# Post-norm attention and ternary feed-forward in one kernel: transpositions over the full array, and the second batch's maxima split one, two, one

## The chip, the cores and the metric

The kernel runs on one core of a Trainium2 chip. The metric is device microseconds (us) of one execution of the program. Five engines work side by side, each through its own instructions in order: TensorE (PE in the profile; its weight loads are listed as PEld), VectorE (DVE), ScalarE (ACT), GpSimd (POOL), and SyncE (SP), which here only issues DMAs. They meet through semaphores.

## The reference

Four batches of 512 tokens, width 512. Attention has 16 heads of 32 dimensions and one key/value head that all of them share; the feed-forward layer has 1408 hidden units and ternary weights.

```python
q = rotary((x @ Wq + bq) per head); k = rotary(x @ Wk + bk); v = x @ Wv + bv
scores = q k^T / sqrt(32); attn = softmax(scores); ctx = attn @ v
x = layernorm(x + ctx @ Wo + bo)
quantize(w) = clip(round(w / (mean|w| + 1e-8)), -1, 1)
hidden = sigmoid(x @ quantize(w1).T) * (x @ quantize(w2).T)
x = layernorm(x + hidden @ quantize(w3).T)
```

The mean in `quantize` is one over a whole weight matrix, so each matrix is read once for its mean and once more to be made ternary, on the chip.

## The kernel before

**Steps.** `T = D = 512` is cut into four chunks of 128 (`NC`, `NT`). A chunk `c` of the query columns holds four heads. The main loop (line 855) goes through 64 steps `n` = (batch `b`, chunk `c`, key tile `t`), 16 to a batch. In step n TensorE makes the scores of 128 keys against 512 queries for four heads (`scores`, two double-bank PSUM tiles `ps` of tag `sc`, with the row maximum subtracted by a second small product), ScalarE takes the exponential (`es`), and TensorE weighs the value rows with the `es` of the step before (`weigh`, into `acc`). The softmax denominators are a further product for the first batch (`count`, into the PSUM bank of tag `den`) and a sum on GpSimd (`total`) for the others.

**Maxima.** The row maxima have to be known ahead. `find_maxima(n + LEAD, ...)` makes them seven steps ahead: for batch 0 with `row_maxima`, for the others with `maximum`, which multiplies the head's queries `qr` with the keys `kr`, one 128x512 product per query chunk, and has VectorE reduce the result (`pmax` to `mx`). `maximum` takes a tile of tag `sc` for two chunks at once, and the single bank of tag `den` for one chunk alone (line 378). After the last chunk of a head group `spread` transposes the 128x16 maxima on TensorE (`pm`), takes them into two float parts (`m`) and sends them round through DRAM to `negm`.

**PSUM.** Tag `sc` has two buffers of two banks, `mm` two of one bank (projections `pk`, `pq`, transposes `pv`, `pm`, `pt`, and the products `po`, `gu` of the later stages), `acc` and `den` one bank each. A buffer is handed on only when its last reader is done, wherever in the program that reader stands: `normalize` copies the denominators out of `den` on ScalarE (`sums<-den`, line 496) some slots after the last `count`.

**Fill.** The engines' order is that of the program text (`pin`). Between the pieces of a step `fill.draw(us)` puts in work of other stages: the input projections of later batches (`project_in`, with the rotation on VectorE: four or five instructions `a`, shuffle, `pq`, `q`), the output projection of the batch before (`project_out`), and its feed-forward layer. Lists of small pieces (`late`, `middle`) come in at `due()`.

**Weights.** `quantize(n)` advances the ternary weights by n tiles: ACT takes the sign of the raw tile (`sgn`), DVE makes the tile of it (`raw<-raw,hi,sgn`), POOL stores it to DRAM (`w<-raw`) and loads the next raw tile. `sgn` lies in SBUF for steps up to 16 and in the PSUM bank `den` after that (line 210). The last tiles are stored just ahead of the first feed-forward product, whose weights (`wg<-w`) take over the buffers of the raw tiles.

**Which steps the loop's two branches take.** While the last batch's input projections are not done (line 876), a step has two pairs of chunks, `find_maxima(.., 0, 1)` and `find_maxima(.., 2, 3)`, both in tag `sc`, with the fill after them. From step 26 on the other branch runs: chunk 0, fill, chunks 1 and 2, fill, chunk 3. Steps 16 to 25 are those of the second batch (b = 1) that fall into the first branch.

## Time and profile before

| what | value |
|---|---|
| median of the runs (lowest, highest) | 672.95 us (667.65, 673.8) |
| the profiled execution itself | 669.15 us, of which the profile spans 667.4 us |
| clock granted to TensorE in it | 0.997 |
| PE busy | 641.6 us, 96% |
| DVE, ACT, POOL busy | 430.4, 282.7, 323.8 us |
| PE, DVE, POOL busy from 160 to 230 us | 66.66, 56.63, 55.97 of 70 us |

Steps 16 to 25 lie between 151.7 and 227.7 us of the profiled execution; the first feed-forward product starts at 239.43 us. In a line of the timeline the columns are the start in us, the time in us, the engine, the line in the kernel, the operation, output<-inputs, their shapes, how many were merged into the line, and in brackets the engine's idle time before it with what ended that. A helper records every operation, so the lines named are those of the helpers (L75, L80, L83, L86) and one goes by the names of the tiles. The clock granted is that of the whole span; per stretch it is in the table of windows.

### The profile page before, as it was taken

What the parts mean: (1) busy time and instruction counts of PE and PEld (TensorE: products, weight loads), DVE (VectorE), ACT (ScalarE), POOL (GpSimd) and SP (SyncE); (2) the same over time, 40 slices, a digit from 0 to 9 for tenths busy, and PEclk for the clock granted to TensorE, in tenths of its full rate; (3) what the DMA queues carried; (4) which work ended last, traced back from release to release, by engine and by line L of the source; (5) the groups of instructions that cost most, each with busy time, mean ns of one, the idle gap of its engine ahead of it and who ended that gap; (6) DMA issues with size and microseconds to landing.
All of it is one profiled execution on the core that took longest, in us unless ns stands there. A gap on an engine that the chain in (4) does not pass through costs nothing.

```text
span 667.4 us, 9352 instructions
## 1 busy us (share of the span) xinstructions
PE 641.6 (96%) x3194; PEld 355.4 (53%) x3194; DVE 430.4 (64%) x619; ACT 282.7 (42%) x441; POOL 323.8 (49%) x414
## 2 busy tenths in 40 slices
PE   8999999999999989999999899999999999999995
PEld 5233333443333445665556465654555685778884
DVE  2987765787886967676666856576535553464345
ACT  2474656564443645333244354232435421234213
POOL 2533344545987766467666265586575702202000
PEclk9999999999999999999999999999999999999998
DMA  8855668777675285454132357451231464237531
GB/s 276 287 170 202 207 193 271 229 242 259 185 235 188 86 263 169 133 179 149 49 106 76 112 163 219 132 157 37 68 105 59 135 222 138 80 110 217 184 105 63
DMA packets 60671, 107.78 MB, mean 162 GB/s; under 512 B 14592, under 2 KB 15360, under 8 KB 60624
## 3 DMA queue, kind: packets, MB, share of 16 engines
q1 hardware_dynamic: 51984, 80.57, 38.9%
q0 software_dynamic: 7920, 25.96, 11.7%
q10 hardware_dynamic: 720, 0.66, 0.3%
q8 instruction: 25, 0.41, 0.3%
q14 instruction: 22, 0.18, 0.1%
HBM read 84.06 MB, written 23.10 MB: 161 GB/s over the span
## 4 chain that ended last, share of the span: by engine, by line
PE 78%; DVE 8%; DMA 5%; ACT 3%; POOL 2%; issue 2%; SPq 1%; ACTq 0%; DVEq 0%; POOLq 0%
PE gu L80 23%; PE po L80 19%; PE ps L80 12%; PE pmax L80 8%; PE acc L80 7%; PE pq L80 6%; DVE mx L75 2%; PE den L80 2%; ACT es L75 2%; DMA xT<-in_xT 2%; POOL total L75 1%; DVE xt L75 1%; DMA wg<-w 1%; DMA bq_sb<-in_bq 1%; DVE part L75 1%
## 5 line engine op out<-in xcount | busy, mean ns | idle before, releaser
L75 DVE TENSOR_REDUCE mx<-pmax 128x1 f32<-128x512 f32 (+1 forms) x159 | 158.2, 1006 | 80.7 <-PE pmax L80 80.4
L75 ACT ACTIVATE es<-ps 128x1024 f32<-128x1024 f32 x128 | 124.2, 1022 | 142.3 <-PE ps L80 134.2
L80 PE MATMUL gu<-y,wg 128*128 128x512 f32 x704 | 172.8, 395 | 1.9 <-DMA wg<-w 0.9
L80 PEld LDWEIGHTS gu<-y,wg 128*128 128x128 f32 x704 | 131.3, 188 | 37.9 <-issue 4.7
L75 POOL TENSOR_TENSOR total<-total,es 128x512 f32<-128x512 f32 x96 | 123.7, 1318 | 45.3 <-ACT es L75 45.2
L80 PE MATMUL po<-wd,h 128*128 128x512 f32 x352 | 87.1, 396 | 4.2 <-DVE y L75 2.9
L75 POOL TENSOR_TENSOR total<-es 128x512 f32<-128x512 f32 x48 | 60.5, 1290 | 56.8 <-ACT es L75 56.8
L80 PE MATMUL pmax<-kr,qr 128*128 128x512 f32 x192 | 75.5, 456 | 3.7 <-ACT es L75 2.2
L80 PEld LDWEIGHTS po<-wd,h 128*128 128x128 f32 x352 | 65.0, 188 | 22.5 <-DVE y L75 4.6
L75 ACT CAST h<-hw 128x512 fp32r<-128x512 f32 x44 | 27.3, 620 | 100.1 <-DVE hw L75 100.1
L80 PE MATMUL acc<-es,v 128*32 128x512 f32 x512 | 68.2, 605 | 0.0
L80 PEld LDWEIGHTS pmax<-kr,qr 128*128 128x128 f32 x192 | 33.7, 188 | 57.3 <-ACT es L75 21.2
L75 DVE SCALAR_TENSOR_TENSOR hw<-th,gu 128x512 f32<-128x512 f32 x44 | 30.2, 686 | 46.8 <-PE gu L80 46.6
L80 PE MATMUL po<-wo_sb,ctxT 128*128 128x512 f32 x128 | 58.9, 593 | 0.3 <-DVE hw L75 0.3
L80 PE MATMUL ps<-negm,ones_r 2*128 2x512 f32 x256 | 58.2, 788 | 0.0
L75 DVE SCALAR_TENSOR_TENSOR xt<-po,xt 128x512 f32<-128x512 f32 x48 | 32.8, 684 | 38.7 <-PE po L80 38.7
L75 DVE TENSOR_TENSOR h<-hw,h 128x512 fp32r<-128x512 f32 x44 | 42.2, 960 | 21.7 <-ACT h L75 21.4
L80 PE MATMUL ps<-qT,kT 32*128 32x512 f32 x384 | 55.7, 640 | 0.0
L75 POOL DMA_DIRECT2D raw<-in_wf x66 | 36.0, 548 | 37.7 <-DMA w<-raw 26.9
L80 PE MATMUL pq<-xT,wq_sb 128*128 128x512 f32 x112 | 53.0, 602 | 1.0 <-ACT v L75 1.0
L75 ACT ACTIVATE th<-gu 128x512 f32<-128x512 f32 x44 | 26.3, 597 | 49.3 <-PE gu L80 49.3
L80 PEld LDWEIGHTS po<-wo_sb,ctxT 128*128 128x128 f32 x128 | 24.1, 190 | 21.9 <-issue 19.6
(98 smaller groups left out, 632.5 us busy)
## 6 DMA issues: line engine op xcount, KB each, us to landing
wg<-w SPq DMA_DIRECT2D x88, 256.0 KB
raw<-in_wf POOLq DMA_DIRECT2D x66, 256.0 KB, 4.4
qr<-qp SPq DMA_DIRECT2D x96, 128.0 KB
wd<-w SPq DMA_DIRECT2D x44, 256.0 KB
w<-raw POOLq DMA_DIRECT2D x33, 256.0 KB, 4.9
qp<-q SPq DMA_DIRECT2D x48, 128.0 KB
rden<-flat SPq DMA_DIRECT2D x64, 64.0 KB
xt<-in_x SPq DMA_DIRECT2D x16, 256.0 KB
```

The lines of the kernel that those rows point to most:

```text
L75: return lambda *args, **kw: pin(getattr(self.engine, name)(*args, **kw))
L80: pin(nc.tensor.matmul(out, lhsT=lhsT, rhs=rhs, start=start, stop=stop))
```

## The change

Three edits:

1. `pv` and `pm` become transpositions over the full array. The value rows were transposed from partitions 96 to 127 alone (32 rows in, 128x32 out); now all 128 rows of `kv` are, 128x128 out, and the copy takes its 32 columns of each. For that `kv` is written on 128 partitions instead of 32. The maxima go to two constant 128x128 tiles, cleared once at the start, and `pm` transposes a whole one instead of its 16 columns.
2. `sgn` of the steps after 16 lies in SBUF, in bfloat16, in the one buffer of tag `rot_a`, instead of the PSUM bank `den`.
3. In steps 16 to 25 the maxima come as chunk 0 (bank `den`), then chunks 1 and 2 together (tag `sc`), and, after 0.3 of the step's fill, chunk 3 (bank `den`).

```diff
                 if now > PER:
-                    sgn = ps_acc.tile([P, W], F32, tag="den", name="sgn")
+                    sgn = work.tile([P, W], BF16, tag="rot_a", name="sgn", bufs=1)
...
         kv = work.tile([P, T], F32, tag="kv", name="kv", bufs=1)
-        act.activation(kv[n:P], pk[n:P], AF.Identity, bias=bkv_sb[n:P, 0:1])
+        act.activation(kv, pk, AF.Identity, bias=bkv_sb[:, 0:1])
...
-                pv = ps_mm.tile([P, NT, HD], F32, tag="mm", name="pv")
+                pv = ps_mm.tile([P, NT, P], F32, tag="mm", name="pv")
                 for t in range(NT):
-                    transpose(pv[:, t, :], kv[n:P, ts(t, P)], ident[n:P, n:P])
+                    transpose(pv[:, t, :], kv[:, ts(t, P)], ident)
                 s.v = work.tile([P, NT, HD], F32, tag="v", name="v", bufs=3)
-                act.copy(s.v, pv)
+                act.copy(s.v, pv[:, :, n:P])
...
+    maxima = [const.tile([P, P], F32, name=f"maxima{k}") for k in range(2)]
+    for tile_ in maxima:
+        pool.memset(tile_, 0.0)
+
+    def room_for_maxima(b, c):
+
+        return maxima[c % 2][:, 0 : NG * NT].rearrange("p (i t) -> p i t", t=NT)
...
-            s.mx[c] = small.tile([P, NG, NT], F32, tag="mx", name="mx")
+            s.mx[c] = room_for_maxima(b, c)
...
-        pm = ps_mm.tile([NG * NT, P], F32, tag="mm", name="pm")
-        transpose(pm, s.mx[c].rearrange("p i t -> p (i t)"), ident)
+        pm = ps_mm.tile([P, P], F32, tag="mm", name="pm")
+        transpose(pm, maxima[c % 2], ident)
+        pm = pm[0 : NG * NT]
...
-        if batches[-1].done < NC:
+        if b == 0:
             find_maxima(n + LEAD, 0, 1)
             begin_middle()
...
             fill.draw(pace)
-            quantize(1 if b == 0 or n % 3 == 0 else 0)
+            quantize(1)
+        elif batches[-1].done < NC:
+
+            find_maxima(n + LEAD, 0)
+            find_maxima(n + LEAD, 1, 2)
+            begin_middle()
+            due()
+            quantize(1)
+            fill.draw(0.3 * pace)
+            find_maxima(n + LEAD, 3)
+            fill.draw(0.7 * pace)
+            quantize(1 if n % 3 == 0 else 0)
```

More of the change, by code (lines that the diff above doesn't have):

```diff
@@ L375, in maximum @@
         if i == 0 and chunks[0] == 0:
-            s.mx[c] = small.tile([P, NG, NT], F32, tag="mx", name="mx")
+            s.mx[c] = room_for_maxima(b, c)
         if len(chunks) == 1:
```

## The prediction

> **What bounds the kernel.** I read the page's first part, then the waits, then the timeline of steps 16 to 27. TensorE is busy for 96% of the span, so a gain must come out of its idle time or its own work.

> ```profile
> PE 641.6 (96%) x3194; PEld 355.4 (53%) x3194; DVE 430.4 (64%) x619; ACT 282.7 (42%) x441; POOL 323.8 (49%) x414
> ```

> ```profile
> 160.00:230.00 70.00, 66.66 (x311) 25.32 (x311) 56.63 (x80) 33.84 (x48) 55.97 (x70) 1.00 0.56 181
> 230.00:240.00 10.00, 7.68 (x50) 4.02 (x47) 9.53 (x15) 5.97 (x9) 9.98 (x11) 1.00 0.79 249
> ```

> ```profile
> PEld pmax L80 <- ACT es L75: 15.6, 19, 1.1
> ```

> The second fence holds the windows of the steps that change and of the stretch behind them; after the length come PE, PEld, DVE, ACT and POOL busy, then the granted clock (1.00, so no term below is a matter of the clock). The last, from the waits of 150 to 240 us, names what the change goes at: the maxima's weight loads wait for the exponentials. Step 19 shows how:

> ```profile
> 177.90 1.06 PE L80 MATMUL acc<-es,v 128*32 128x512 f32 x8
> 179.13 0.73 PE L80 MATMUL pmax<-kr,qr 128*128 128x512 f32 x2 [0.17 <-ACT es L75]
> 180.05 0.74 PE L80 MATMUL pmax<-kr,qr 128*128 128x512 f32 x2 [0.18 <-ACT es L75]
> 180.63 1.88 PE L80 MATMUL pq<-xT,wq_sb 128*128 128x512 f32 x4
> ```

> Undisturbed, `acc` hands over after 0.88 us (127.54 to 128.42), and four `pmax` take 1.03 us (129.40 to 130.43), 0.26 each. Here 178.78 to 180.63 is 1.85: an excess of 0.82. Each pair waits for a `sc` bank, the first 1.08 us after the exponentials start, the second 2.00. The excess in steps 18 to 25 is 0.76, 0.82, 0.73, 0.72, 0.84, 0.83, 0.82 and 0.70, in sum 6.2. Step 16 has none, and in step 17 `pk` waits for an `xT` load that ends at 165.29 anyway.

> **Part 3, the split maxima.** Chunk 0 would start when `acc` is through, and the pair follows as soon as the first exponential frees its bank (about 0.1 later than chunk 0 ends). If nothing else held, eight steps would give 6.2 - 8 x 0.1 = 5.4 us. But both single chunks use the one bank `den`, so each needs the reduction of the one before, and VectorE takes those in program order. I laid each step's instructions on each engine in the changed order, with the durations of this trace, and found four places where the bank is late.

> Step 16: the last `count` stands directly ahead of chunk 0, and its copy `sums<-den` on ACT, behind two `es` and `ctxT`, ends at 156.23. Chunk 0 starts at 156.31 instead of 155.27: 1.04 lost, nearly all absorbed in step 17 by the `xT` wait. Step 18 starts 0.16 late.

> Steps 17, 18 and 19: chunk 3's reduction stands on VectorE behind a whole rotation.

> ```profile
> 167.21 0.75 DVE L75 SCALAR_TENSOR_TENSOR a<-pk,bkv_sb,cos_sb 96x512 f32<-96x512 f32 x1 [0.93 <-ACT kv L75]
> ...
> 169.40 1.38 DVE L75 TENSOR_TENSOR kT<-a,pk 96x512 f32<-96x512 f32 x2
> ```

> In step 17 the rotation ends at 170.78, the reduction (0.68) at 171.46, and step 18's chunk 0, wanted at 170.45, starts at 171.52: the whole gain of step 18 gone. In step 18 it ends about when step 19 wants it. In step 19 the reduction ends near 185.6, or 186.5 with the next part's cost, and step 20 wants the bank at 184.1: 1.4 to 2.4 lost. From step 20 on chunk 3's reduction stands ahead of the slow work, and steps 21 to 24 gain 0.6 to 0.8 each. In step 25 chunk 3 follows `pm` with no fill between, and waits 0.7 for chunk 0's reduction.

> VectorE also gets more to do: two reductions of 0.68 and one of 1.215 for two of 1.215, +0.145 a step, 1.45 in ten. The orders of ACT, POOL and SP stay as they are, so no DMA is moved past another; the later release of a `qr` buffer by chunk 3 (about 2 us) is hidden, since five buffers leave its next load two steps.

> **Part 2, signs in SBUF.** ACT's write costs 0.72 instead of 0.69. The reader is the matter: `raw` then has two tensor inputs in SBUF, as `h` has, and `h` shows what that does beside GpSimd.

> ```profile
> 259.13 5.03 POOL L75 TENSOR_TENSOR total<-total,es 128x512 f32<-128x512 f32 x4 [2.79 <-ACT es L75]
> ```

> ```profile
> 126.12 0.92 DVE L75 SCALAR_TENSOR_TENSOR raw<-raw,hi,sgn 128x512 f32<-128x512 f32 x1
> ...
> 203.09 0.74 DVE L75 SCALAR_TENSOR_TENSOR raw<-raw,hi,sgn 128x512 f32<-128x512 f32 x1
> ...
> 263.01 1.70 DVE L75 TENSOR_TENSOR h<-hw,h 128x512 fp32r<-128x512 f32 x1
> ...
> 536.32 0.69 DVE L75 TENSOR_TENSOR h<-hw,h 128x512 fp32r<-128x512 f32 x1 [0.69 <-ACT h L75]
> ```

> Alone `h` takes 0.69; under a running `total` it takes 1.70, one GpSimd instruction (1.24) longer. `raw` with `sgn` in SBUF took 0.92 next to a GpSimd product at 126.12; with `sgn` in PSUM it took 0.72 to 0.75 all through 160 to 229, though GpSimd was busy. Of the 12 `raw` after step 16, eight fall under `total`: between nothing and 8 x 1.1 = 8.8; I take 8 x 0.85 = 6.8, most `h` under `total` being near 1.7. VectorE's load from 160 to 230 then goes from 56.6 to 56.6 + 1.45 + 6.8 = 64.9 of 70 us. Most of that fills VectorE's waits for `pmax`; it shows on the path where a reduction or rotation queues behind it, in steps 19 to 20 (0.9) and 25 to 27 (1.4).

> **The sum of parts 2 and 3.** Starts of the score products against before, by step: 18 +0.2, 19 +0.2, 20 -0.5, 21 +1.2, 22 +0.8, 23 +0.1, 24 -0.7, 25 -1.4, 26 -1.0. Then VectorE, 9.53 of 10 us busy from 230 to 240, decides: its rotation starts 0.4 later than before, and TensorE's `pt` and scores go with it (+0.45). TensorE then waits 0.91 less for the first weights, since their chain (POOL `q` at 229.40, store at 230.62, load at 235.50) starts about 1.4 earlier. First `gu`: 239.0 instead of 239.43, -0.4. From there all is the same order as before, and TensorE-bound; the shift stays.

> **Part 1, full-width transpositions.** `pm` and `pv` become what `pt` is: weight load 140 ns for 88 and 136, matmul 273 for 272 and 222.

> ```profile
> 135.72 0.73 PE L80 MATMUL pmax<-kr,qr 128*128 128x512 f32 x2
> 136.29 0.27 PE L86 MATMUL pm<-ident,mx 128*16 128x128 f32 x1
> 136.31 0.71 PE L80 MATMUL pmax<-kr,qr 128*128 128x512 f32 x2
> ...
> 173.89 0.43 PE L86 MATMUL pv<-ident,kv 32*128 32x32 f32 x4
> ```

> The two `pmax` pairs with `pm` between take 1.14 up to `pq` (136.86), without it 1.03: 0.11 for a narrow `pm`. Four `pt` take 0.60 to 0.66, so about 0.11 apiece in a stream. `pm` is between nothing and 16 x 0.052 = 0.83 dearer; I take 0. Four `pv` take 0.43 and would take 0.60: at most 4 x 0.17 = 0.7, and I take 0.2, since in step 18 chunk 3 lies behind them and fills the wait for ACT's copy. A gain of the size of that copy's wait (0.35, twice) is the other end. `kv` on 128 partitions is 0.68 before and 0.69 by the row `r`; the two clearings (0.2 each) lie on POOL at the start, ahead of loads that the critical chain does not hold.

> [...]

> **Together** -0.4 + 0.2 = -0.2 us on the profiled 669.15, 668.95. The runs of before lie at 667.65, 669.15 (profiled), 672.95 and 673.8; their mean is 670.9, and I set the forecast on it: about 671, 2 below the median. The three runs scatter by 0.9%, so a change under 1% (6.7 us) can't be told from none.

> **Rivals.** (a) VectorE keeps up and the bank is free: the 5.4 come whole, with the last wait for weights shortened too, 669.15 - 5.4 - 0.9 = 662.9, up to 1% faster. For it: PE's wait is plain, and VectorE waited 6.9 us for `pmax` in 160 to 230. Against it: the rotation ahead of chunk 3's reduction in steps 17 to 19. Chance 0.17.
> (b) Slower, through VectorE as the bound of steps 17 to 27: at 8.8 instead of 6.8 for the signs its work is 66.9 of 70 us, and once the 3 us left are less than its own waits for `pmax`, 6.9 before, of which half stay, it sets the step: +0.4 to +4, or 669.5 to 673. It decides from about 1.0 us extra per `raw`, with two more on the path. Chance 0.25.
> (c) Chunk 3 waits at each step, because the fill draws less than VectorE needs for chunk 0's reduction: 0.7 as in step 25 in each of ten, +7, 676. Against it: two `pq` or `po` rows give 1.7. Chance 0.05.
> (d) The forecast, within about 2 of no change: 0.53.

> **Range and chances.** On the mean 670.9, (a) reaches to 665, (b) to 675; the runs' own scatter adds 2 above: 665 to 676, and the forecast's own range 668 to 674. Faster by over 1% is the far part of (a), 0.05; slower by over 1% is (c) and the end of (b), 0.08; within 1%, 0.87.

> **What would show it.** After: a wait of the first `pmax` of steps 18 and 20 that ends with VectorE's reduction, not with `es`; chunk 0 of step 16 behind `sums<-den`; `raw` at 1.4 to 1.8 where `total` runs; `po` of steps 21 to 23 half a microsecond behind the pair instead of 1.5 us behind `acc`; first `gu` near 239. I am wrong if VectorE's order lets the reductions pass earlier, if `raw` stays at 0.74, or if the narrow transpositions cost more than 0.11 by a wait that this trace puts down to other rows.

## The result, and the profile after

| | before | after |
|---|---|---|
| median of the runs (lowest, highest) | 668.99 us (667.42, 673.8), 22 runs | 672.19 us (668.89, 675.94), 22 runs |
| ratio, 95% interval | | 1.0040 [1.0025, 1.0055] |
| profiled execution, its span, its granted clock | 669.15, 667.4 us, 0.997 | 673.71, 671.9 us, 0.993 |

The change makes the kernel slower, by 2.7 us of 669 (1.7 to 3.7). The ratio is not that of the two medians; the means, 672.24 and 669.54 us, give it. The forecast was -0.2 us. The time measured lies between the 665 and 676 us that were given, but the change goes the other way.

The engines and the granted clock by slices, from the page of after:

```profile
PE 641.5 (95%) x3194; PEld 358.3 (53%) x3194; DVE 440.1 (65%) x629; ACT 283.1 (42%) x441; POOL 327.5 (49%) x416
...
PEclk9999999999979999999999999999999999999999
```

VectorE has 9.7 us more to do, TensorE as much as before, but one slice of the clock row shows a 7. The windows of after place it (length, then PE, PEld, DVE, ACT and POOL busy, then the granted clock, DMA share, GB/s):

```profile
160.00:230.00 70.00, 64.31 (x290) 26.71 (x289) 62.50 (x84) 31.48 (x44) 54.51 (x67) 0.95 0.55 174
230.00:240.00 10.00, 7.48 (x41) 3.26 (x40) 8.67 (x13) 6.58 (x10) 9.98 (x10) 1.00 0.51 148
...
184.10:187.50 3.40, 1.78 (x16) 0.32 (x10) 3.27 (x7) 2.42 (x3) 3.40 (x3) 1.00 0.27 103
187.50:194.30 6.80, 6.15 (x10) 3.20 (x11) 4.92 (x6) 1.24 (x2) 4.11 (x6) 0.50 0.71 198
194.30:197.70 3.40, 3.40 (x24) 1.06 (x22) 1.91 (x5) 0.56 (x1) 0.00 (x0) 1.00 1.01 374
```

From 187.5 to 194.3 us TensorE has half its clock, with 1.00 on both sides. TensorE's timeline of after, steps 16 to 21, shows what stands ahead of that:

```profile
156.27 0.96 PE L80 MATMUL pmax<-kr,qr 128*128 128x512 f32 x3 [0.93 <-ACT sums L75]
...
171.89 0.97 PE L80 MATMUL pmax<-kr,qr 128*128 128x512 f32 x3 [1.71 <-DVE maxima L75]
...
184.82 1.06 PE L80 MATMUL acc<-es,v 128*32 128x512 f32 x8
188.15 1.65 PE L80 MATMUL pmax<-kr,qr 128*128 128x512 f32 x3 [2.27 <-DVE maxima L75]
189.60 3.62 PE L80 MATMUL po<-wo_sb,ctxT 128*128 128x512 f32 x4
```

The waits of 150 to 240 us no longer have a row of `pmax` behind `es`. They have this one:

```profile
PEld pmax L80 <- DVE maxima L75: 13.2, 10, 3.2
```

So the waits for exponentials are gone, and waits for VectorE's reduction of the one bank stand in their place. In the timeline above, the third line from below is the last product before the wait of step 20; the `po` behind it takes 3.62 us, where four such products of `pq` at 172.69, at a clock of 1.00, took 1.88. VectorE's timeline of after shows what the reduction stood behind:

```profile
174.17 2.40 DVE L75 SCALAR_TENSOR_TENSOR raw<-raw,hi,sgn 128x512 f32<-128x512 f32 x1
...
183.40 1.25 DVE L75 SCALAR_TENSOR_TENSOR raw<-raw,hi,sgn 128x512 f32<-128x512 f32 x1
184.57 0.74 DVE L75 SCALAR_TENSOR_TENSOR a<-pq,bq_sb,cos_sb 128x512 f32<-128x512 f32 x1
...
186.81 0.69 DVE L75 TENSOR_TENSOR q<-a,pq 128x512 f32<-128x512 f32 x1
187.41 0.68 DVE L75 TENSOR_REDUCE maxima<-pmax 128x1 f32<-128x512 f32 x1
...
207.22 4.06 DVE L75 SCALAR_TENSOR_TENSOR raw<-raw,hi,sgn 128x512 f32<-128x512 f32 x1
```

The rotation, from `a` at 184.57 to `q`, stands right ahead of the reduction (`maxima`), with a `raw` ahead of both.

Starts of the score products against before, in us. The runs start up to 1.5 us apart for reasons of their own, so each row is taken from its own step 16:

| step | before, start | after | ten products in step 20's wait | signs made on ScalarE | the same, reduction first |
|---|---|---|---|---|---|
| 17 | 159.83 | +1.00 | +0.99 | +1.02 | +1.03 |
| 18 | 168.11 | -0.31 | +0.43 | +0.49 | +1.63 |
| 20 | 182.44 | +0.47 | -0.03 | -0.07 | +0.35 |
| 21 | 189.92 | +5.75 | +1.58 | +0.48 | -0.28 |
| 26 | 227.73 | +4.21 | +0.02 | -2.35 | -2.05 |
| first `gu` | 239.43 | +4.74 | +0.61 | -2.52 | -1.94 |

In the column of after little is lost up to step 20, 5.3 us between the starts of steps 20 and 21, and 1.5 is won by step 26.

### The profile page after: what moved, and what is told of

Read it like the earlier page. It is cut to its first block, busy times and chain, and to the rows that moved or that the text cites. A ratio compares the mean times of both kernels' runs of the same rounds, so it can differ in the third digit from the quotient of the medians.

```text
span 671.9 us, 9356 instructions
## 1 busy us (share of the span) xinstructions
PE 641.5 (95%) x3194; PEld 358.3 (53%) x3194; DVE 440.1 (65%) x629; ACT 283.1 (42%) x441; POOL 327.5 (49%) x416
## 4 chain that ended last, share of the span: by engine, by line
PE 80%; DVE 14%; DMA 2%; ACT 2%; issue 1%; ACTq 0%; DVEq 0%
PE gu L80 23%; PE po L80 19%; PE ps L80 12%; PE pmax L80 9%; PE acc L80 8%; PE pq L80 6%; DVE maxima L75 4%; PE den L80 2%; DVE raw L75 2%; DVE xt L75 1%; DVE part L75 1%; DMA bq_sb<-in_bq 1%; PE pk L80 1%; DVE y L75 1%; DMA xT<-in_xT 1%
## 5 line engine op out<-in xcount | busy, mean ns | idle before, releaser
L75 DVE TENSOR_REDUCE maxima<-pmax 128x1 f32<-128x512 f32 (+1 forms) x169 | 159.2, 955 | 79.2 <-PE pmax L80 78.9
L75 ACT ACTIVATE es<-ps 128x1024 f32<-128x1024 f32 x128 | 124.2, 1022 | 145.9 <-PE ps L80 138.6
L80 PE MATMUL gu<-y,wg 128*128 128x512 f32 x704 | 172.5, 395 | 1.9 <-DMA wg<-w 0.9
L80 PEld LDWEIGHTS gu<-y,wg 128*128 128x128 f32 x704 | 131.2, 188 | 37.3 <-issue 4.4
L75 POOL TENSOR_TENSOR total<-total,es 128x512 f32<-128x512 f32 x96 | 124.5, 1330 | 42.9 <-ACT es L75 42.8
L75 POOL TENSOR_TENSOR total<-es 128x512 f32<-128x512 f32 x48 | 61.4, 1309 | 60.7 <-ACT es L75 60.7
L80 PE MATMUL po<-wd,h 128*128 128x512 f32 x352 | 86.9, 395 | 4.2 <-DVE y L75 3.0
L80 PE MATMUL pmax<-kr,qr 128*128 128x512 f32 x192 | 78.3, 471 | 7.9 <-DVE maxima L75 6.9
L80 PEld LDWEIGHTS po<-wd,h 128*128 128x128 f32 x352 | 64.9, 188 | 22.3 <-DVE y L75 4.6
L75 ACT CAST h<-hw 128x512 fp32r<-128x512 f32 x44 | 27.3, 620 | 99.8 <-DVE hw L75 99.8
L80 PE MATMUL acc<-es,v 128*32 128x512 f32 x512 | 68.2, 605 | 0.0
L80 PEld LDWEIGHTS pmax<-kr,qr 128*128 128x128 f32 x192 | 35.0, 191 | 60.6 <-DVE maxima L75 19.4
L80 PE MATMUL po<-wo_sb,ctxT 128*128 128x512 f32 x128 | 61.8, 611 | 0.3 <-DVE hw L75 0.3
L75 DVE SCALAR_TENSOR_TENSOR hw<-th,gu 128x512 f32<-128x512 f32 x44 | 30.2, 686 | 46.7 <-PE gu L80 46.6
L75 DVE SCALAR_TENSOR_TENSOR xt<-po,xt 128x512 f32<-128x512 f32 x48 | 32.8, 684 | 38.6 <-PE po L80 38.6
L80 PE MATMUL ps<-negm,ones_r 2*128 2x512 f32 x256 | 57.8, 788 | 0.0
L75 DVE TENSOR_TENSOR h<-hw,h 128x512 fp32r<-128x512 f32 x44 | 42.0, 956 | 21.7 <-ACT h L75 21.4
L80 PE MATMUL ps<-qT,kT 32*128 32x512 f32 x384 | 56.2, 640 | 0.0
L75 POOL DMA_DIRECT2D raw<-in_wf x66 | 36.0, 548 | 36.8 <-DMA w<-raw 25.9
L80 PE MATMUL pq<-xT,wq_sb 128*128 128x512 f32 x112 | 53.2, 601 | 0.7 <-ACT v L75 0.5
L75 ACT ACTIVATE th<-gu 128x512 f32<-128x512 f32 x44 | 26.3, 597 | 49.2 <-PE gu L80 49.1
L80 PEld LDWEIGHTS po<-wo_sb,ctxT 128*128 128x128 f32 x128 | 24.9, 196 | 22.1 <-issue 19.1
```

What stands on the lines that cost most here:

```text
L75: return lambda *args, **kw: pin(getattr(self.engine, name)(*args, **kw))
L80: pin(nc.tensor.matmul(out, lhsT=lhsT, rhs=rhs, start=start, stop=stop))
```

## Experiments

The theory after the result: step 20's wait makes the granted clock fall, and both together take what the split maxima win. Rivals: the wider transpositions cost more than shown; the signs in SBUF alone do it; the split order in itself is worth nothing. Every ratio is to runs of before on the same chip, with its 95% interval.

### Each part alone

Before with edit 1 alone, with edit 2 alone, and with edit 3 alone (the signs then stay in `den`):

```diff
+        pm = ps_mm.tile([P, P], F32, tag="mm", name="pm")
+        transpose(pm, maxima[c % 2], ident)
...
+                    sgn = work.tile([P, W], BF16, tag="rot_a", name="sgn", bufs=1)
...
+            find_maxima(n + LEAD, 0)
+            find_maxima(n + LEAD, 1, 2)
```

> The kernel before with the full-width transpositions alone. Both theories (the granted clock falls after step 20's wait; or the waits alone make the loss) put nothing on this part: the scores of step 16 start at 151.69 us in the changed kernel and at 151.68 before, behind three of the four pv and six of the sixteen pm. Expected: ratio 0.999 to 1.001, pm at 0.27 us each, and the clock at 1.00 throughout. The rival that the transpositions cost what their weight loads and matmuls add would give +0.8 to +1.5 us, 1.001 to 1.002.

> The kernel before with the signs of steps after 16 in SBUF alone, maxima in two pairs as before. Raw tiles should take 1.2 to 2.4 us under total, in sum about 9 us more of VectorE's time between 160 and 230 us. Theory of the clock: the pairs' buffers are freed by the exponentials and the reductions of the step before, no wait of TensorE passes 2 us, the clock stays at 1.00, and the first gu is 0 to 1.5 us later: ratio 1.000 to 1.002. [...]

> Before, with only the split order of the maxima in steps 16 to 25; the signs stay in the den bank, the transpositions stay narrow. Of each step the single chunks now share den with the signs: ACT's sign pass waits for a reduction, and the next single chunk waits for raw. If signs in SBUF were a cost and no more, this order alone keeps the gain that the changed kernel with signs made on ScalarE showed: ratio 0.996 to 0.999, clock 1.00 in 185 to 196. If they are needed so that the split can work, chunk 0 of step 16 to 20 waits 1 us or more for den behind sign and raw, the clock falls at one of these waits, and the ratio is 1.002 to 1.010.

| kernel | median | ratio |
|---|---|---|
| transpositions alone | 670.05 us | 0.9999 [0.9979, 1.0020] |
| signs in SBUF alone | 671.0 us | 1.0021 [1.0002, 1.0039] |
| split maxima alone | 678.16 us | 1.0128 [1.0107, 1.0148] |
| all three | 672.19 us | 1.0040 [1.0025, 1.0055] |

The transpositions cost nothing that can be measured. In the profiled execution of the signs alone the twelve `raw` take some 5 us more, not the 9 expected, and the clock falls for 3.4 us at 236.1 us, where TensorE waits 1.22 and 1.07 us ahead of transpositions (against the expectation, which had it hold while no wait passes 2 us); the mean clock of its runs is 0.9935, that of before beside it 0.996. The parts don't add up: 0.0 + 0.2 + 1.3 is far above 0.4. The split order alone is the dearest, above both of its expected ranges, since signs and single chunks then share `den`. TensorE's timeline of the split maxima alone:

```profile
190.49 0.47 PE L80 MATMUL pmax<-kr,qr 128*128 128x512 f32 x1 [1.60 <-DVE raw L75]
...
233.36 0.77 PE L80 MATMUL pmax<-kr,qr 128*128 128x512 f32 x1 [3.73 <-DVE raw L75]
```

Chunk 3 waits for `raw` to have read the signs, seven times, by 0.48 to 3.73 us, and in the last of these waits, at 232.2 us, the clock falls for 6.8 us. So the signs in SBUF are dear by themselves (0.2%) and worth 0.9% beside the split maxima, which need `den` for themselves. I had priced that edit as a cost only.

### TensorE kept busy in step 20's wait

The changed kernel with ten 128x128 products that nobody reads, ahead of step 20's chunk 0:

```diff
+            if n == 20:
+                busy = ps_mm.tile([P, P], F32, tag="mm", name="busy")
+                for _ in range(10):
+                    mm(busy, ones, ones, True, True)
```

> The changed kernel with ten products of 128x128 into an unread tile ahead of step 20's first chunk: they keep TensorE at work for some 2.3 us of the time in which it waits for the bank. They leave the wait itself as it is: chunk 0 still starts at about 188.2 us. Theory of the clock: it stays at 1.00 in 185 to 196 us (0.69 in the changed kernel), step 21 starts at about 192.7 instead of 195.7, and the ratio falls from 1.004 to 0.999 to 1.001. Theory of the waits alone: nothing changes, 1.004, or worse by what the products delay.

Measured: 670.92 us, ratio 1.0016 [0.9997, 1.0035]. Its window over the same stretch of steps:

```profile
185.00:196.00 11.00, 11.00 (x56) 5.82 (x55) 9.99 (x15) 4.50 (x8) 8.26 (x10) 1.00 0.71 220
```

The clock stays at 1.00, and step 21 starts 1.58 us late where it was 5.75. The bank is still late, as TensorE's and VectorE's timelines of this kernel show:

```profile
183.03 1.07 PE L80 MATMUL acc<-es,v 128*32 128x512 f32 x8
184.03 2.50 PE L80 MATMUL busy<-ones 128*128 128x128 f32 x20
186.28 0.95 PE L80 MATMUL pmax<-kr,qr 128*128 128x512 f32 x3
```

```profile
185.18 0.68 DVE L75 TENSOR_REDUCE maxima<-pmax 128x1 f32<-128x512 f32 x1
```

The reduction ends at 185.86, 1.8 us behind `acc` where it was 2.2 in after, and the products end 0.4 later still. So what fell away is for the most part what the halved clock cost. The ratio is higher than expected: the mean clock over this kernel's runs is 0.994, so it falls in other runs too; where, no trace shows.

### Step 19's chunk 3 right behind its pair

```diff
+            if n == 19:
+                find_maxima(n + LEAD, 3)
             quantize(1)
             fill.draw(0.3 * pace)
-            find_maxima(n + LEAD, 3)
+            if n != 19:
+                find_maxima(n + LEAD, 3)
```

> The changed kernel with chunk 3 of step 19 alone put directly behind the pair, ahead of the fill, so that its reduction stands ahead of the rotation. Theory of the clock: step 20's wait for the bank (2.3 us) goes to under 0.4, the clock stays at 1.00, and step 21 starts 5 us earlier, near 190.5; ratio 0.996 to 0.999. Theory of the waits alone: 2.3 us are gained, less 0.3 for chunk 3's own wait, 1.001. If the clock falls at the next long wait instead (step 18's is 1.7 us), the ratio stays above 1.001 too, and the window shows where.

Measured: 670.47 us, ratio 1.0018 [0.9997, 1.0038]. Two of its windows:

```profile
185.00:196.00 11.00, 11.00 (x45) 5.01 (x45) 10.93 (x14) 5.41 (x9) 10.00 (x12) 1.00 0.67 216
230.00:240.00 10.00, 7.45 (x39) 3.73 (x39) 8.06 (x14) 4.55 (x7) 7.74 (x8) 0.83 0.84 259
```

Chunk 3 itself waits 0.32 us, step 20's wait is gone, and step 26 starts 1.5 us early by its own step 16. Then TensorE waits 1.38 and 1.07 us for the rotation and for `y` ahead of step 26's transpositions, and at 234.5 us the clock halves for 3.4 us. The gain was made, and given back a few steps on. Waits of 1.39 and 1.07 us stand at the same place in the executions of after and of the ten products, where the clock held. Over the twelve runs of this kernel the clock is no higher than in after (0.992 against 0.993), though step 20's wait is gone. So step 20 is not the only place where VectorE's lateness lowers the clock, and only one execution of each kernel shows where it fell.

### VectorE relieved, and VectorE put in another order

Four kernels run together. The first two make the ternary tile by two ScalarE passes (rounding by adding a large constant, then the sign), so that VectorE has no `raw` after step 16: on before, and on the changed kernel. The third issues chunk 3's product and reduction from within the fill, ahead of the rotation. The fourth is the second and third together.

```diff
-                    sgn = work.tile([P, W], BF16, tag="rot_a", name="sgn", bufs=1)
+                    act.activation(raw, raw, AF.Identity, bias=magic, scale=inv[m])
+                    act.activation(raw, raw, AF.Sign, bias=minus)
...
-                act.activation(sgn, raw, AF.Sign, bias=hi[m])
-                dve.scalar_tensor_tensor(raw, raw, hi[m], sgn, ALU.is_gt, ALU.min)
+                    act.activation(sgn, raw, AF.Sign, bias=hi[m])
+                    dve.scalar_tensor_tensor(raw, raw, hi[m], sgn, ALU.is_gt, ALU.min)
...
+            while pending:
+                pending.pop()()
             rotation = turn(
...
+            pending.append(lambda k=n + LEAD: find_maxima(k, 3))
             fill.draw(0.3 * pace)
-            find_maxima(n + LEAD, 3)
+            while pending:
+                pending.pop()()
```

> Before, with the ternary tiles behind step 16 made by two ACT passes in place, so that VectorE has no raw operation there and no tile of signs is needed: 12 VectorE instructions of 0.74 us less, ACT's pass for the sign is kept (0.69) and one more pass of about 0.7 us comes for each. It is the base for the next run: it shows what the ternary step costs in itself. Both theories (VectorE blocked by GpSimd; TensorE's wait that lowers the clock) expect nothing on the path: clock 1.00 in 160 to 240, steps 18 to 26 within 0.5 us of before, ratio 0.998 to 1.002. If ACT is the cover that is missing (56.6 less, 33.8 of 70 us busy before, so it should not be), steps come later by up to 0.7 each where an exponential queues behind the extra pass, 1.003 or more.

> The changed kernel, with the same two ACT passes in the place of raw: transpositions and split maxima as they are, but nothing on VectorE that reads two SBUF tiles for the ternary step (18.2 us of raw go from VectorE). If the signs' extra 9.3 us on VectorE are what made step 20's bank so late: TensorE's wait there falls from 2.4 to 1.4 us or less (the rotation of step 19 remains ahead of the reduction), the clock stays at 1.00 in 185 to 196, step 21 starts within 1 us of before instead of 5.8 late, steps 25 and 26 are 1 to 2 us early, ratio 0.995 to 1.000. If the order of the split maxima alone does it: the wait stays at 2 us or more, the clock falls, step 21 is 4 us or more late, ratio 1.002 to 1.006.

> The changed kernel, with chunk 3's product issued where TensorE has the fill's products behind it, but with its reduction on VectorE ahead of the rotation of that fill in steps 17 to 19 and later ones, signs in SBUF as they are. If the rotation ahead of the reduction is what makes the bank late: the waits of chunk 0 in steps 18 and 20 (1.71 and 2.27 us) go to 0.5 or less, the clock stays at 1.00 in 185 to 196, steps 21 to 26 come 0 to 2 us earlier than before, ratio 0.996 to 1.001. The rotation then ends 0.7 us later for each step, and may make the weights of steps 26 and 27 late: if a wait of 1 us or more stands there, the clock falls in 230 to 240 as it did with step 19's chunk moved alone, and the ratio is 1.001 to 1.003. If the raws' waits decide whatever the order is, a wait of over 1.5 us remains in steps 18 to 22 and the ratio is 1.002 or more.

> Both of the above: no raw on VectorE and chunk 3's reduction ahead of the rotation. If VectorE's lateness, through TensorE's waits and the clock, is the whole reason why the split maxima gave nothing, the gain that the excess of 6.2 us promised should show here: no wait of TensorE for a reduction above 1 us in steps 18 to 26, clock 1.00 from 160 to 240, step 26 3 to 5 us earlier than before, ratio 0.992 to 0.997. If something else takes the place of the wait (ACT, the store and load of q, the first weights), step 26 is early by 2 us or more but the first hidden layer's product is not, and the ratio is 0.998 to 1.002.

| kernel | median | ratio | step 20's wait |
|---|---|---|---|
| before, signs made on ScalarE | 671.49 us | 0.9998 [0.9976, 1.0021] | |
| changed, signs made on ScalarE | 668.02 us | 0.9964 [0.9944, 0.9985] | 1.11 us |
| changed, reduction ahead of rotation | 669.01 us | 0.9977 [0.9956, 0.9998] | none; 1.12 us a step earlier |
| changed, both | 665.31 us | 0.9931 [0.9908, 0.9954] | none |

On before the other way to make the signs is worth nothing, so it isn't a gain that merely comes along. On the changed kernel it takes 0.76% off, the order 0.63%, both 1.1%. The last kernel is 4.6 us (3.1 to 6.2) faster than before, 0.7%, and so faster than the changed kernel too. Its windows:

```profile
160.00:230.00 70.00, 67.28 (x321) 27.62 (x321) 54.01 (x85) 44.29 (x61) 58.64 (x73) 1.00 0.63 190
230.00:240.00 10.00, 7.08 (x47) 3.96 (x46) 8.14 (x13) 5.11 (x8) 9.98 (x11) 1.00 0.86 269
```

VectorE is busy for 54.0 of 70 us where after had 62.5, and the clock holds. The share of each: in the second kernel step 20's wait falls from 2.27 to 1.11 us, so about half of it came from `raw`; the order alone removes it whole, so the two shares overlap. The expectation for step 26 (3 to 5 us early) was too high: 2.05 by its own step 16. TensorE waited 1.4 us for `xT` in step 17 of this execution, 0.25 in that of the second kernel. From step 18 to step 26 it wins 3.7 us on before.

The third kernel has no wait above 1.4 us in these steps, and its profiled execution still has the lowest clock of the four. Its TensorE timeline, and its windows:

```profile
182.58 0.49 PE L80 MATMUL pmax<-kr,qr 128*128 128x512 f32 x1 [1.12 <-DVE maxima L75]
...
235.65 1.11 PE L86 MATMUL pt<-ident,xt 128*128 128x128 f32 x4 [1.39 <-DVE q L75]
```

```profile
185.00:196.00 11.00, 11.00 (x44) 3.99 (x40) 9.61 (x15) 4.53 (x6) 6.84 (x8) 0.72 0.64 180
230.00:240.00 10.00, 7.64 (x45) 4.50 (x48) 9.23 (x13) 4.98 (x8) 9.98 (x11) 0.78 0.66 192
```

Two falls of 6.8 us behind waits of 1.1 and 1.4. My expectation of 1.00 in 185 to 196 was wrong for this execution (673.99 us); other runs of the kernel, at a clock of 0.998, take 667.0 to 668.8 us. So the length of one wait doesn't decide alone, and the last three kernels ask what does.

### What a wait of TensorE costs beyond its own length

Before, with a wait put in by hand in steps 19, 21 and 23: a product that nobody reads waits for one (hold_a), five (hold_b) or nine (hold_c) copies in a row on ScalarE.

```diff
+            if n in (19, 21, 23):
+                late_ = work.tile([P, P], F32, tag="late", name="late_", bufs=1)
+                act.copy(late_, es[1][:, 1, 0:P])
+                for _ in range(4):
+                    act.copy(late_, late_)
+                held = ps_mm.tile([P, P], F32, tag="mm", name="held")
+                mm(held, ones, late_, True, True)
```

> Before, with a wait put on TensorE by hand ahead of the maxima of steps 19, 21 and 23: one unread 128x128 product whose right side is a ScalarE copy (128 columns) of the second exponentials. Estimate from the rows of before: the second exponentials end some 1.1 us behind acc, the copy takes about 0.3, so TensorE waits 1.3 to 1.5 us in one piece, and the pairs of maxima behind it no longer wait (0.8 saved). Cost of the waits alone: 3 x 0.8 = 2.4 us, ratio 1.003 to 1.004. If a wait of that size can lower the clock (as one of 1.13 us did in the run with the reduction ahead of the rotation), 0.50 stands for 3.4 or 6.8 us behind one or more of the three, each 1.7 or 3.4 us dearer: ratio 1.005 to 1.010.

> The same with four more copies in a row on ScalarE: the wait is some 1.2 us longer, 2.5 to 2.8 us. By the waits alone 3 x 2.0 = 6 us, ratio 1.008 to 1.010; with the clock lowered behind each of them 6 us plus 5 to 10, ratio 1.015 to 1.024.

> The same with eight more copies: 3.6 to 4.0 us of wait. By the waits alone 3 x 3.2 = 9.6 us, ratio 1.013 to 1.016; with the clock lowered behind each 9.6 us plus 5 to 10, ratio 1.020 to 1.030. Across the three runs: if what a wait costs beyond its own length grows with its length from 1.4 to 3.8 us, the clock goes by how much of a stretch TensorE was idle; if it is the same from 1.4 on, any wait of over one microsecond is enough.

The second of the three waits, from TensorE's timelines of hold_a, hold_b and hold_c:

```profile
195.74 0.49 PE L80 MATMUL held<-late__1811,ones 128*128 128x128 f32 x2 [1.42 <-ACT late__1811 L75]
```

```profile
197.66 0.79 PE L80 MATMUL held<-late__1815,ones 128*128 128x128 f32 x2 [2.74 <-ACT late__1815 L75]
```

```profile
203.11 0.80 PE L80 MATMUL held<-late__1819,ones 128*128 128x128 f32 x2 [4.05 <-ACT late__1819 L75]
```

| | wait | ratio | falls of the clock behind the three | loss from step 19 to 26 |
|---|---|---|---|---|
| hold_a | 1.42 us | 1.0034 [1.0016, 1.0053] | none | 3.1 us |
| hold_b | 2.73 us | 1.0182 [1.0150, 1.0213] | two, 3.4 us each | 10.3 us |
| hold_c | 4.05 us | 1.0231 [1.0211, 1.0250] | three, 6.8, 3.4 and 3.4 us | 16.2 us |

The first wait of hold_b, behind which the clock held, makes step 20 2.31 us later; the two others 3.96 and 4.02, so a fall of 3.4 us costs 1.7. By that, three waits alone would be 6.9 us in hold_b. In hold_c they would be 3 x 3.6 = 10.8 (2.31 and the 1.31 that the wait is longer), and the clock takes the other 5.4. In these executions the clock fell behind none of the waits of 1.42 us, two of three of 2.73, and all three of 4.05. The runs without a trace don't show that the price goes on growing: by the ratios, 669.7 us of before, and the 6.9 and 10.8 us of the waits alone, the clock took about 5.3 us in hold_b and 4.7 in hold_c, and nothing in hold_a (2.3 in all). The mean clocks agree: 0.9955 in hold_a, 0.986 in hold_b, 0.985 in hold_c, 0.996 in before beside them.

## Why the prediction was wrong

**The step that failed** is "the granted clock (1.00, so no term below is a matter of the clock)". That was read off before, where no wait in TensorE's timeline of steps 16 to 25 is above 0.4 us, and carried over to a kernel for which the same text forecast a wait of 1.4 to 2.4 us in step 20. The wait came at 2.27, and near its end the clock halved for 6.8 us. Keeping TensorE busy in that wait brings step 21 from 5.75 to 1.58 us late; my forecast for it was 1.2.

How much of the 2.7 us that is over all runs: where the granted clock of the whole run is above 0.9955, after takes 670.03 us on average (4 of 22 runs) and before 669.56 (51 of 81, those beside the experiments). So at a high clock the change is worth some +0.5, against my -0.2; four runs, 668.9 to 671.4 us, are too few to tell these two apart. At or below 0.9935 are 16 of the 22 runs of after, and 13 of 81 of before. The rest, about 2 us, goes with the clock. That 672.19 lies so near the forecast of 671 is luck: the forecast was set on 670.9, the mean of the four runs of before then known, and the mean of the 22 is 669.5.

**Step 16 to 18: right.** Chunk 0 of step 16 at 156.27 behind `sums` (forecast 156.31), taken up by the wait for `xT`; step 18's chunk 0 behind the rotation at 171.89 (171.52).

**Step 20: mechanism right, size at the upper end.** The reduction was to end at 185.6 to 186.5; it ended at 188.09, behind the rotation as forecast. TensorE was ready for the bank at 185.88, not 184.1, so the wait of 2.27 us stays inside the forecast 1.4 to 2.4. The wait was priced at its length alone.

**The signs: mis-sized.** "One GpSimd instruction longer", 8 x 0.85 = 6.8 us, 8.8 at most. Measured: the twelve `raw` take 18.2 us for 8.8, 9.3 more. In the three other kernels profiled with the split order and the same `raw` it is 7.1 (ten products), 8.0 (chunk 3 moved) and 10.0 (reduction first). In after the eight `raw` that meet a `total` on GpSimd take 0.85 to 4.06 us, the four others 0.71 to 0.75. What the price left out is that the wait can be longer than one instruction: two of the twelve waited 1.7 and 3.3 us, 5.0 of the 9.3. At 207.22 `raw` takes 4.06 us, and GpSimd's timeline of after has four `total` in a row there:

```profile
205.78 4.94 POOL L75 TENSOR_TENSOR total<-total,es 128x512 f32<-128x512 f32 x4
```

Four take 1.24 each and end at 210.72; `raw` alone is 0.74, so it ran from about 210.5, when the row was through: it waited for three of them. That the one who waits gets in after one GpSimd instruction, as I had priced it from the 1.70 us of `h`, is not what the 4.06 us show.

**Transpositions: right**, 0.9999 where I had +0.2 us.

**Steps 21 to 26: half right.** With the clock held by the ten products, step 26 is at +0.02 (forecast -1.0) and the first `gu` at +0.61 (-0.4): step 21 starts 0.4 later than forecast, and 1.6 us are won from there to step 26, not 2.2. The sum for the signs isn't the reason, since in that execution the `raw` took 7.1 us more, near my 6.8; which term is short stays open. With no `raw` on VectorE 2.8 us are won.

**The rivals.** Rival (b), VectorE as the bound, has the measured change in its range (+0.4 to +4) and names the right engine; but TensorE lost its time in one long wait and the clock behind it, not in steps that VectorE sets. Rival (a), the whole gain of 5.4 us, was no mirage: with VectorE relieved at both places the runs show 4.6 us of it. I had named both places, and taken them for small losses.

## What to carry to other kernels

Where a change takes many short waits of TensorE and leaves one long one, price the long one above its length: here three waits of 1.4 us put in by hand cost no more than their length, and three of 2.7 or 4 us some 5 us more. It is no safe limit, since behind waits of 1.1 and 1.4 us the clock fell for 6.8 us each in the kernel with the reduction first. A single buffer that two users share in turn is only as early as the last reader's queue lets it be (here `den`: its reduction stood behind a rotation, and TensorE waited 2.27 us); move its reader ahead of the long work on that engine, or take work off the engine, before the split order is judged. And measure parts together as well as alone: the signs' move cost 0.2% by itself and was worth 0.9% beside the split.

## What the runs showed of the hardware that I had not expected

The grid's first point, worked back by the estimated step, lies 0.06 to 3.15 us behind the start of the span in these ten executions. That this makes much of the scatter of the times is likely but not shown; what is shown is that over the 81 runs of before that stand beside the experiments the time goes with the granted clock (correlation -0.74), 669.6 us on average above 0.9955 and 673.6 at or below 0.9915. What else a stretch has to hold for a fall, since 0.95 us was enough in one place and 1.42 not in another, stays open.
